# Moving a partial sum two places later in a hand-ordered scan kernel, and fetching one of its inputs a group earlier

## The chip, the cores and the metric

The kernel runs on one NeuronCore of a Trainium2 chip. A NeuronCore has five engines that run their own instruction streams and meet only at semaphores: TensorE (PE, matrix multiplies and transposes into PSUM), VectorE (DVE), ScalarE (ACT), GpSimd (POOL), and SyncE (SP), whose queue issues all the DMA transfers of this kernel. The metric is the device time of one execution in microseconds (us). Three executions of the kernel before gave a median of 11595.92 us (11591.5 to 11607.49). The profile is one further execution, which took 11561.61 us.

## The reference

The input is a batch of eight images of 96 channels, 64 by 64. The first layer is a vision state-space block: layer norm, a projection to 192 inner channels with a depthwise convolution, a selective scan over the 4096 pixels in four directions, a gate, a projection back, and a small convolutional branch. The second layer is linear attention and a quantized feed-forward part. Nearly all the time lies in the scan, which for each of 8 images, 4 directions, 192 channels and 16 states runs 4096 steps:

```python
def step(h, inp):
    u_t, d_t, b_t, c_t = inp
    dA = jnp.exp(d_t[..., None] * A)
    h = dA * h + (d_t * u_t)[..., None] * b_t[:, :, None, :]
    y = jnp.einsum('bkdn,bkn->bkd', h, c_t)
    return (h, y)
...
y = out_y[:, 0] + inv_y[:, 0] + wh_y + invwh_y      # the four directions, added
```

So a scan output is a sum over 16 states, and the final `y` is a sum over four directions (row order, column order, and both reversed). Everything before and after the scan (norms, convolutions, gate, attention, feed-forward) is the "lane" work below.

## The kernel before, in words

**Units, groups, jobs.** Images are taken in four pairs p (NP = 4). A pair has 384 channels, three tiles T of 128 (T = 0, 1: one image each; T = 2: the last 64 channels of both). A job is one pair, one direction k, one chunk of CH = 1024 pixels and one tile T: 192 jobs. A job has four groups j, each of 32 channels; a group g has four units q, each of 128 partitions holding 32 channels by 4 states. That is 768 groups and 3072 units. The first pair takes the directions in the order k = 0, 2, 1, 3, the other pairs 1, 3, 0, 2. Directions 2 and 3 are the reversed ones.

**What a group does.** The names are those of the profile's tiles:

- `spread(g)`: two 128x512 matmuls copy 32 channels of `du` (delta times u) to 128 partitions in the PSUM tile `pu`. There is one `pu`, so the matmuls of group g+1 wait until VectorE has read `pu` for group g.
- `weave(g)`: in three of four groups of T = 0 and in all of T = 1, eight 128x128 transposes of tiles `turned` make the scan input of unit 0 directly in the PSUM tile `pb0`. The `turned` tiles are made by ScalarE: 32 multiplications 128x128 a job, issued in `spin(job)`.
- `decay(u)`: ScalarE's exponential `da`, 128x1024, one a unit; four buffers.
- `scan(u)`, called for pairs of units (q = 0 and q = 2): VectorE multiplies `pu` by `bm` into `pb` (not for a woven unit), then runs two scans of 128x1024 into a tile `hc`; POOL copies the carry and multiplies `hc` by `cm`, in place, 128x2048. There are four `hc` buffers, so two groups' worth.
- `total(g)`: the partial sum. 16 matmuls of 32x256 (in the trace 32, as a float32 matmul runs as two passes) add the four states on the partitions of all four units into `yp`, the left half of the PSUM bank `yps`. In the reversed directions (k = 2, 3) a first matmul with the identity adds the sums of the opposite direction, fetched into `prev`; in k = 2 of the pairs 1 to 3 another adds the turned sums of the column directions, fetched into `yet`. ScalarE copies `yp` to `y`, and one DMA (k < 2) or four (k >= 2) store it.
- `before(g)`: the fetches of `prev` (384 in all) and `yet` (144), one buffer each.

**The order is written out by hand.** `InOrder` (L254 to L280; nearly every instruction is recorded from L266) chains every instruction of PE, DVE, ACT and POOL to the one before it on that engine, so each engine runs them in the order of the program's calls. SP issues DMAs in program order too, and blocks where one has to wait for its buffer or its data.

**Slots.** `Slots.run()` is a tick: it runs what is due at this tick, then lets each generator ("lane") of other work take one step. A group has six ticks: one before the scan of the first pair, two after it, and the same for the second pair; a job has 24, and `at` is the tick modulo 24. The ticks of a group are called slots 1 to 6 here. Lanes get PE and ACT time by a budget (`RATE`, 1.4 and 1.25 us a tick). They write to two PSUM banks only, bank 0 (`pg`) and bank 1 (`yps`, shared with `total`); `take` hands out a free bank and keeps bank 1 away from lanes in the ticks between a partial sum and its copy. `steps(job)` prepares the next job: at tick 5 and 6 of each job it uses both banks for the delta projection, each with a softplus on ACT. `left_at`, `there` and `turned` hold back work whose inputs another lane is still making; if an input is missing at the start of a job, the loop runs 24 ticks of lanes alone, with no scan between.

**The order around the change.** The main loop (L1494 to L1543) does, for a group g:

1. slot 1; `scan` of the first pair; fetches of `bm` and `cm` for later units; `decay` for the second pair; `total(g-1)`;
2. slot 2 (the copy of `yp`, `after(1)`), slot 3;
3. slot 4; `scan` of the second pair; fetches; `decay` for the next group's first pair; `spread(g+1)`, `weave(g+1)`;
4. slot 5, slot 6 (the store of `y`, `after(5)`); then in slot 1 of the next group `before(g)`, so that `prev` for `total(g)` is fetched right before it.

So between `pu` of group g and `pu` of group g+1 PE's queue holds: the transposes of g, the lane matmuls of slots 5, 6 and 1, `total(g-1)`, the lane matmuls of slots 2, 3 and 4.

Of the kernel before, what the change touches and what calls it, by code (L numbers as in the profile page):

```python
# [9 lines left out]
F32 = mybir.dt.float32  # L10
# [272 lines left out]
RING, EXTRA = 7, 1  # L283


class Slots:
# [24 lines left out]
    def take(self, pe, act, long=0, first=False):  # L311
        while True:
            at = self.at % 24
            if long:
                if (
                    self.at % 6 in (5, 0)[: 1 + (long == 2)] and min(self.left) > -2
                    and 0 not in self.held and not at <= 6 < at + long and not self.wanted
                ):
                    self.hold(0)
                    self.pay(pe, act)  # L320
                    i = 0
                    return self.banks[i]
            elif first or min(self.left) > 0:
                free = [
                    i for i in range(2)
                    if i not in self.held and self.at > self.last
                    and not (i == 1 and at % 6 in (1, 2)) and at != (5, 4)[i]
                ]
                if free:
                    i = min(free, key=lambda i: self.used[i])  # L330
                    self.hold(i)
                    self.pay(pe, act)
                    return self.banks[i]
            yield
# [40 lines left out]
def phase_b(  # L375
# [8 lines left out]
    with ExitStack() as ctx:  # L384
# [80 lines left out]
        slots = Slots(bank0, yps)  # L465
# [20 lines left out]
        def woven(job):  # L486

            return jobs[job][3] < 2

        def weaves(u):  # L490

            job, j, q = units[u]
            return q == 0 and woven(job) and not (j == 0 and jobs[job][3] == 0)
# [5 lines left out]
        def steps(job):  # L499

            p, k, ci, c, T, at = where(job)
            if T == 0:

                sts[job // 3] = gp.tile([80, 512], F32, name="st")
                r0, r1 = 64 + R * (k // 2), 32 * (k // 2)
                for i, hs in enumerate(halves):
                    for b in range(2):
                        for to, n, r in ((32 * i + R * b, R, r0), (64 + 8 * i + 4 * b, 4, r1)):
                            nc.sync.dma_start(
                                sts[job // 3][to : to + n, :],  # L510
                                xd_d[k % 2][2 * p + b][r : r + n, at][:, hs],
                            )
            dtw = gp.tile([32 + 2 * R, 128], F32, name="dtw")
            for i in range(2):
                nc.sync.dma_start(dtw[32 * i : 32 * i + 2 * R, :], a["dtw"][:, k, T, :])
            dus[job] = gp.tile([128, CH], F32, name="du", bufs=2)
            nc.sync.dma_start(dus[job], xi_d[k % 2][p][T][:, at])
            yield
            while slots.at % 24 != 5:
                yield  # L520
            dl = gp.tile([128, CH], F32, name="turned", bufs=RING)
            for i, hs in enumerate(halves):
                bank = slots.banks[1 - i]
                assert 1 - i not in slots.held
                slots.hold(1 - i)
                slots.pay(0.9, 2.5)
                rows = slice(32 * i, 32 * i + 2 * R)
                pe.matmul(bank, dtw[rows, :], sts[job // 3][rows, :], start=True, stop=True)
                se.activation(dl[:, hs], bank, AF.Softplus, bias=dtb[:, k, T : T + 1])
                slots.give(bank)  # L530
                if i:
                    exps()
                else:
                    yield
            ge.tensor_mul(dus[job], dus[job], dl)
            yield from wait(2)
            nc.sync.dma_start(dl_d[k][p][T][:, at], dl)
            if woven(job):
                assert slots.spun is None
                slots.spun = spin(job)  # L540
            yield

        def spin(job):


            turns[job], b, slots.wanted = [], jobs[job][3], True
            dt = gp.tile([128, 8, 128], F32, name="turned", bufs=RING)
            for i in range(2):
                bank = yield from slots.take(0.6, 0.6, first=True)
                for x in range(4):  # L550
                    pe.transpose(
                        bank[:, 128 * x : 128 * x + 128],
                        dus[job][:, 512 * i + 128 * x : 512 * i + 128 * x + 128],
                        ident,
                    )
                se.copy(dt[:, 4 * i : 4 * i + 4, :], bank)
                slots.give(bank)
                yield
            if b == 0:
                bts[job // 3] = gp.tile([128, 4, 2, 8], F32, name="bt", bufs=2)  # L560
                bank = yield from slots.take(0.5, 0.3, first=True)
                for x in range(4):
                    pe.transpose(
                        bank[:, 16 * x : 16 * x + 16],
                        sts[job // 3][64:80, 128 * x : 128 * x + 128],
                        ident[64:80, 64:80],
                    )
                se.copy(bts[job // 3], bank[:, 0:64])
                slots.give(bank)
                yield  # L570
            bt, slots.wanted = bts[job // 3], False
            nxt = slots.at
            while len(turns[job]) < 4:
                n, at = len(turns[job]), slots.at % 24
                if slots.at < nxt or (job and woven(job - 1) and n >= EXTRA and 6 < at < 17):
                    yield
                    continue
                nxt = slots.at + 3
                slots.pay(0.0, 2.4)
                t = gp.tile([128, 2, 128, 4], F32, name="turned", bufs=RING)  # L580
                for i in range(2):
                    for m in range(4):
                        x, c = 2 * n + i, 4 * b + m
                        scale = bt[:, x % 4, x // 4, c : c + 1]
                        se.mul(t[:, i, :, m], dt[:, x, :], scale)
                turns[job].append(t)
                yield

        def weave(g):

# [803 lines left out]
        def spread(g):  # L1394
            job, j, _ = units[4 * g]
            for hs in halves:
                pe.matmul(pu[:, hs], sel[:, j, :], dus[job][:, hs], start=True, stop=True)
# [29 lines left out]
        def before(g):  # L1427


            job, j, _ = units[4 * g]  # L1430
            p, k, ci, c, T, at = where(job)
            if k >= 2:
                prevs[g] = wp.tile([128, 256], F32, name="prev", bufs=1)
                nc.sync.dma_start(prevs[g], ya_d[k % 2][p][T][c, j])
            if k == 2 and p > 0:
                assert p in turned
                yet[g] = wp.tile([128, 256], F32, name="yet", bufs=1)
                nc.sync.dma_start(
                    yet[g],
                    ys_d[0][p][T][32 * j : 32 * j + 32, at].rearrange("r (i x) -> i r x", i=4),  # L1440
                )

        def total(g):
# [30 lines left out]
                        y[32 * i : 32 * i + 32, :],  # L1474
                    )

            slots.after(1, lambda: se.copy(y, yp))
            slots.after(5, store)

        slots.first = steps(0)  # L1480
        while not slots.idle():
# [12 lines left out]
        for u in range(0, n, 2):  # L1494
            g, q = divmod(u, 4)
            if q == 0:
                if g % 4 == 0:
# [11 lines left out]
                            slots.lanes.append(columns(p))  # L1509
                    if p == NP - 1 and k == 2:  # L1510
                        if ci == 0 and T == 1:
                            assert not slots.lanes
                            slots.lanes += [last_gate(), last_rest(0), last_rest(1)]
                        if ci > 0 and T == 0:
                            left_at[ci - 1] = slots.at + 15
                    if job < len(jobs):
                        p, k, ci, c, T, at = where(job)
                        while (p, k % 2, c) not in there:
                            for _ in range(24):
                                slots.run()  # L1520
                        slots.first = steps(job)
# [7 lines left out]
                weights(v, 1)  # L1529
            for v in range(u + 2, min(u + 4, n)):  # L1530
                decay(v)
            if q == 2:
                if g + 1 < n // 4:
                    spread(g + 1)
                    if weaves(4 * g + 4):
                        weave(g + 1)
            elif g > 0:
                total(g - 1)
            slots.run()
            slots.run()  # L1540
            if q == 2:
                slots.after(1, lambda g=g: before(g))
        slots.run()  # L1543
        slots.run()
# [501 lines left out]
```

## Time and profile before

| | |
|---|---|
| median of three runs | 11595.92 us |
| profiled execution, device time | 11561.61 us |
| its span, first to last instruction | 11559.5 us |
| DVE busy | 10092.0 us (87%) |
| POOL busy | 8645.6 us (75%) |
| PE busy (weight loads apart) | 8426.8 us (73%) |
| ACT busy | 7949.4 us (69%) |
| DMA queue, share of 16 engines | 49.6% |
| granted TensorE clock, mean | 0.824 |
| first and last scan start | 224.4 and 11224.9 us |

Each row of the page's fifth part is one kind of instruction on one engine: its tiles as out<-in, its count, its busy time in all and the mean of one, then the engine's idle time just before such instructions, with what ended it. The list of waits sums the same idle time by who waited for whom. In the timeline a line is a run of like instructions: start, length, engine, name, and in brackets the idle time before it.

### The profile page before, as it was taken

What the parts mean: (1) busy time and instruction counts of PE and PEld (TensorE: products, weight loads), DVE (VectorE), ACT (ScalarE), POOL (GpSimd) and SP (SyncE); (2) the same over time, 40 slices, a digit from 0 to 9 for tenths busy, and PEclk for the clock granted to TensorE, in tenths of its full rate; (3) what the DMA queues carried; (4) which work ended last, traced back from release to release, by engine and by line L of the source; (5) the groups of instructions that cost most, each with busy time, mean ns of one, the idle gap of its engine ahead of it and who ended that gap; (6) DMA issues with size and microseconds to landing.
All of it is one profiled execution on the core that took longest, in us unless ns stands there. A gap on an engine that the chain in (4) does not pass through costs nothing. (4 is left out here: it accounts for less than half of the span.)

```text
span 11559.5 us, 135952 instructions
## 1 busy us (share of the span) xinstructions
PE 8426.8 (73%) x44332; PEld 3637.9 (31%) x44332; DVE 10092.0 (87%) x6202; ACT 7949.4 (69%) x13591; POOL 8645.6 (75%) x3961
## 2 busy tenths in 40 slices
PE   7867787666687777766677787777767766666778
PEld 3323333222233333333233333333322333222333
DVE  4898999999788899978988889997998989899874
ACT  3657776555777777768777777666876767875664
POOL 2687778777877778877777777878777878877760
PEclk8877887777788888878788888888888888877889
DMA  3454544544645556564444455656444655544551
GB/s 117 141 195 157 160 155 169 174 132 145 202 148 162 161 157 199 180 201 151 147 143 142 149 166 158 204 172 201 154 148 152 163 162 176 183 143 134 165 150 38
DMA packets 902259, 1836.80 MB, mean 159 GB/s; under 512 B 248990, under 2 KB 422239, under 8 KB 894511
## 3 DMA queue, kind: packets, MB, share of 16 engines
q1 hardware_dynamic: 901550, 1828.11, 49.6%
q8 instruction: 352, 5.77, 0.2%
q14 instruction: 357, 2.92, 0.1%
HBM read 1407.23 MB, written 420.42 MB: 158 GB/s over the span
## 5 line engine op out<-in xcount | busy, mean ns | idle before, releaser
L266 POOL TENSOR_TENSOR hc<-hc,cm 128x2048 f32<-128x2048 f32 x1536 | 6970.2, 4538 | 729.4 <-DVE hc L266 410.5
L266 DVE TENSOR_TENSOR_SCAN hc<-da,carry,pb 128x1024 f32<-128x1024 f32 x2304 | 5274.9, 2332 | 259.0 <-ACT da L266 244.6
L266 DVE TENSOR_TENSOR pb<-pu,bm 128x1024 f32<-128x1024 f32 x2624 | 3101.8, 1221 | 796.4 <-PE pu L266 733.6
L266 ACT ACTIVATE da<-dl,c_alog 128x1024 f32<-128x1024 f32 x3072 | 3356.4, 1141 | 120.6 <-DVE hc L266 116.2
L266 PE MATMUL yp<-hc,c_add 128*32 128x256 f32 x24576 | 1989.3, 467 | 1028.5 <-POOL hc L266 801.6
L266 PE MATMUL pu<-du,c_sel 128*128 128x512 f32 x3072 | 1969.5, 775 | 486.3 <-DVE pb L266 485.4
L266 DVE TENSOR_TENSOR_SCAN hc<-da,pb 128x1024 f32<-128x1024 f32 x768 | 1711.6, 2271 | 92.8 <-ACT da L266 84.8
L266 PEld LDWEIGHTS yp<-hc,c_add 128*32 128x32 f32 x24576 | 812.7, 128 | 2227.6 <-POOL hc L266 1068.4
L266 ACT ACTIVATE turned<-turned,bt 128x128 f32<-128x128 f32 x4096 | 1321.1, 509 | 0.0
L266 POOL COPY carry<-hc 128x2 f32<-128x2 f32 x1152 | 215.6, 187 | 1296.4 <-DVE hc L266 1221.9
L266 PEld LDWEIGHTS pu<-du,c_sel 128*128 128x128 f32 x3072 | 688.9, 241 | 1405.3 <-issue 707.5
L266 ACT COPY y<-yp 128x256 f32<-128x256 f32 x768 | 280.9, 366 | 1177.1 <-PE yp L266 1173.4
L266 POOL TENSOR_TENSOR u<-u,u 96x512 f32<-96x512 f32 (+1 forms) x474 | 595.1, 1261 | 212.0 <-ACT u L266 207.1
L266 ACT ACT_TABLE_LOAD x566 | 726.2, 1283 | 34.9 <-DMA cb<-y 13.9
L266 ACT COPY u<-pg 128x512 f32<-128x512 f32 (+5 forms) x492 | 270.7, 550 | 592.4 <-PE pg L266 520.8
L266 PE MATMUL yp<-prev,ident 128*128 128x256 f32 x768 | 312.3, 495 | 481.5 <-DMA prev<-ya 288.9
L266 PEld LDWEIGHTS pb<-ident,turned 128*128 128x128 f32 x3584 | 483.4, 158 | 352.5 <-issue 237.3
L266 POOL TENSOR_TENSOR du<-du,turned 128x1024 f32<-128x1024 f32 x192 | 454.2, 2366 | 164.2 <-ACT turned L266 164.0
L266 PE MATMUL pb<-ident,turned 128*128 128x128 f32 x3584 | 528.4, 296 | 13.3 <-DVE hc L266 13.2
L266 PEld LDWEIGHTS yp<-prev,ident 128*128 128x128 f32 x768 | 156.9, 233 | 785.6 <-issue 291.0
L266 ACT COPY u<-yp 96x512 f32<-96x512 f32 (+6 forms) x252 | 138.8, 551 | 362.0 <-PE yp L266 264.3
L266 PE MATMUL pg<-ain,wmain 96*128 96x512 f32 x792 | 375.2, 613 | 6.3 <-ACT u L266 4.5
(350 smaller groups left out, 8591.2 us busy)
## 6 DMA issues: line engine op xcount, KB each, us to landing
dl<-dl SPq DMA_DIRECT2D x768, 512.0 KB
bm<-xd SPq DMA_DIRECT2D x512, 512.0 KB
cm<-xd SPq DMA_DIRECT2D x512, 512.0 KB
du<-xi SPq DMA_DIRECT2D x192, 512.0 KB
dl<-turned SPq DMA_DIRECT2D x192, 512.0 KB
ya<-y SPq DMA_DIRECT2D x384, 128.0 KB
prev<-ya SPq DMA_DIRECT2D x384, 128.0 KB
xi<-u SPq DMA_DIRECT2D x152, 256.0 KB
```

Source lines behind the costliest of these rows:

```text
L266: op(*args, **kw)
```

## The change

`total(g-1)` is called at the end of the first half of group g, behind slot 3 and not in front of slot 2. The copy of `yp` comes two slots after it and not one (slot 5), the store six and not five (slot 3 of the next group). `before(g)` is called in slot 4 of group g, right behind `total(g-1)`, and not in slot 1 of group g+1. The bank rules follow: bank 1 is kept from lanes in ticks 3, 4 and 5 of six, not in 1 and 2, and the delta projection at tick 5 and 6 takes bank 0 first, not bank 1. The 32 multiplications of a woven job are issued by fours, one four a tick (one every second tick for T = 0), not by eights every third tick. Two loops that run lanes alone are added: before k = 2 of a pair if its `turned` sums are not there, and before the last pair's T = 1 of k = 2 if lanes are left.

```diff
@@ Slots.take
-                    and 0 not in self.held and not at <= 6 < at + long and not self.wanted
+                    and 0 not in self.held and not at <= 5 < at + long and not self.wanted
...
-                    and not (i == 1 and at % 6 in (1, 2)) and at != (5, 4)[i]
+                    and not (i == 1 and at % 6 in (3, 4, 5)) and at != (4, 5)[i]
@@ steps(job)
-                bank = slots.banks[1 - i]
-                assert 1 - i not in slots.held
-                slots.hold(1 - i)
+                bank = slots.banks[i]
+                assert i not in slots.held
+                slots.hold(i)
@@ spin(job)
-            nxt = slots.at
-            while len(turns[job]) < 4:
-                n, at = len(turns[job]), slots.at % 24
-                if slots.at < nxt or (job and woven(job - 1) and n >= EXTRA and 6 < at < 17):
-                    yield
-                    continue
-                nxt = slots.at + 3
-                slots.pay(0.0, 2.4)
-                t = gp.tile([128, 2, 128, 4], F32, name="turned", bufs=RING)
-                for i in range(2):
-                    for m in range(4):
-                        x, c = 2 * n + i, 4 * b + m
-                        scale = bt[:, x % 4, x // 4, c : c + 1]
-                        se.mul(t[:, i, :, m], dt[:, x, :], scale)
-                turns[job].append(t)
-                yield
+            for x in range(8):
+                while job and woven(job - 1) and x >= 2 * EXTRA and 6 < slots.at % 24 < 17:
+                    yield
+                if x % 2 == 0:
+                    t = gp.tile([128, 2, 128, 4], F32, name="turned", bufs=RING)
+                slots.pay(0.0, 1.2)
+                for m in range(4):
+                    c = 4 * b + m
+                    scale = bt[:, x % 4, x // 4, c : c + 1]
+                    se.mul(t[:, x % 2, :, m], dt[:, x, :], scale)
+                if x % 2:
+                    turns[job].append(t)
+                yield
+                if b == 0:
+                    yield
@@ before(g)
-                assert p in turned
@@ total(g)
-            slots.after(1, lambda: se.copy(y, yp))
-            slots.after(5, store)
+            slots.after(2, lambda: se.copy(y, yp))
+            slots.after(6, store)
@@ the main loop
-                            assert not slots.lanes
+                            while slots.lanes:
+                                for _ in range(24):
+                                    slots.run()
...
+                    while k == 2 and p > 0 and p not in turned:
+                        for _ in range(24):
+                            slots.run()
...
-            if q == 2:
-                if g + 1 < n // 4:
-                    spread(g + 1)
-                    if weaves(4 * g + 4):
-                        weave(g + 1)
-            elif g > 0:
-                total(g - 1)
+            if q == 2 and g + 1 < n // 4:
+                spread(g + 1)
+                if weaves(4 * g + 4):
+                    weave(g + 1)
             slots.run()
             slots.run()
-            if q == 2:
+            if q == 0:
+                if g > 0:
+                    total(g - 1)
                 slots.after(1, lambda g=g: before(g))
```

## The prediction

> **What bounds the kernel now.** First the page's busy times, then its costliest groups, then the list of waits, then one stretch of the timeline. From the page:
>
> ```profile
> L266 DVE TENSOR_TENSOR_SCAN hc<-da,carry,pb 128x1024 f32<-128x1024 f32 x2304 | 5274.9, 2332 | 259.0 <-ACT da L266 244.6
> L266 DVE TENSOR_TENSOR pb<-pu,bm 128x1024 f32<-128x1024 f32 x2624 | 3101.8, 1221 | 796.4 <-PE pu L266 733.6
> L266 DVE TENSOR_TENSOR_SCAN hc<-da,pb 128x1024 f32<-128x1024 f32 x768 | 1711.6, 2271 | 92.8 <-ACT da L266 84.8
> ```
>
> VectorE does the scans and sets the pace: these rows are 10088 of its 10092 us. The last column is what can be won at all: 796.4 + 259.0 + 92.8 = 1148 us of idle time, 734 of it for `pu`, 329 for `da`. Two stretches of the page by windows show both ends, DVE busy 199 us of 200 where lanes are few, 144 where the fetches of `yet` are added:
>
> ```profile
> core 0: us, PE busy (x) PEld busy (x) DVE busy (x) ACT busy (x) POOL busy (x), PEclk, DMA share, GB/s
> 2400.00:2600.00 200.00, 120.57 (x684) 52.40 (x684) 199.06 (x116) 106.24 (x161) 153.82 (x66) 0.75 0.39 129
> 5000.00:5200.00 200.00, 147.19 (x725) 61.68 (x726) 143.84 (x85) 116.77 (x205) 146.24 (x90) 0.81 0.59 192
> ```
>
> The list of waits says who is late. PE, in order, stands before the partial sum `yp` for POOL's `hc` and for `prev` and `yet`; ACT stands before the copy `y`:
>
> ```profile
> ACT y L266 <- PE yp L266: 1173.4, 412, 12.1
> PEld yp L266 <- POOL hc L266: 1068.4, 427, 12.2
> PE yp L266 <- POOL hc L266: 801.6, 320, 11.7
> DVE pb L266 <- PE pu L266: 733.6, 282, 11.3
> DVE hc L266 <- ACT da L266: 329.4, 190, 26.8
> PE yp L266 <- DMA prev<-ya: 288.9, 51, 16.7
> PE yp L266 <- DMA yet<-ys: 48.2, 27, 7.3
> ```
>
> The timeline of one late group ties these together:
>
> ```profile
> 5000.28 4.45 DVE L266 TENSOR_TENSOR_SCAN hc<-da,pb 128x1024 f32<-128x1024 f32 x2
> 5001.33 1.22 PE L266 MATMUL yp<-prev,ident 128*128 128x256 f32 x2 [3.15 <-DMA prev<-ya]
> 5003.55 1.22 PE L266 MATMUL yp<-yet,ident 128*128 128x256 f32 x2 [1.00 <-DMA yet<-ys]
> 5004.70 3.01 PE L266 MATMUL yp<-hc,c_add 128*32 128x256 f32 x32
> 5007.65 1.10 PE L266 MATMUL pg<-u,c_centre 96*96 96x512 f32 x2
> ...
> 5009.91 1.10 PE L266 MATMUL yp<-u,mean 96*96 96x512 f32 x2 [1.17 <-ACT u L266]
> ...
> 5010.85 1.88 PE L266 MATMUL pu<-du,c_sel 128*128 128x512 f32 x4
> ...
> 5012.77 1.23 DVE L266 TENSOR_TENSOR pb<-pu,bm 128x1024 f32<-128x1024 f32 x1 [8.03 <-PE pu L266]
> ```
>
> PE stood 4.15 us for the two fetches, ran the sum, then 3.2 us of lane work (slots 2 to 4), and only then `pu`; DVE had been done since 5004.73. PE's stop lies in front of lane work that needed none of what it waited for.
>
> **The change part by part.** *PE.* From the two programs' orders, each lane matmul priced by the timeline's 0.43 us between passes of 512 columns, a group has 4.19 us of lane matmuls on PE in both. Before, 2.49 stand ahead of the sum and 1.70 between sum and `pu`; after, 3.87 and 0.32. So 1.38 us a group, 81% of what lies between, goes in front of the sum, into the stop. I read for every group from the trace's records: when PE was free ahead of the sum, when the sum ended, when `pu` began, when POOL's `hc` ended. 294 groups have a late `pu` (734 us). In these, from the start of the first pair's scans, PE was free at 2.3 us, `hc` ended at 2.8, the sum at 7.65 though its matmuls need some 2.0 (32 passes took 1.93 at 9389.81), `pu` began at 11.9, and DVE was done at 11.8. The new start of `pu` is then the later of (free + 81% of the lane stretch + 2.0, and 0.4 to 0.7 for the identity matmuls) and (`hc` end + 1.1 for the second half), plus 19% of the lane stretch. Per group, and never more than its wait, this gives 390 us of the 734; in 124 groups the wait goes wholly. Bounds: 0, if the lane matmuls moved ahead find their own inputs late, and 734.
>
> The discount: the lane stretch of a late group is 4.24 us long with 3.27 busy, so 0.97 waits, mostly for ACT; run earlier, they may wait longer. A quarter of the gain, 100 us; ends 0 and 294 x 0.97 x 0.81 = 231.
>
> What is late next is PE itself: in 127 groups lanes, sum, `pu` and transposes add to more than the 12.88 us that a group takes where DVE is never idle (48 groups in 618 us, 2226 to 2845), by 160 us together. That stays in any order.
>
> *The fetches (SP).* `prev` and `yet` are asked for a group's length ahead and not in the same slots; their 289 + 48 us on PE are part of the 390. 384 and 144 transfers move three slots up SP's queue; each waits there until `total(g-1)` has read its buffer. SP's wait for that is 456.1 us in 213 cases before, 2.1 each. Queued behind it are `bm`, `cm`, `dl`, lane loads and stores; POOL waits for `cm` (103.2 us, 41 times) and ACT for lane loads. They are needed a pair or more later (6.7 us in a quiet group), so I take 0, ends -50 and +100.
>
> *ACT.* The copy of `yp` goes behind the two `da` of the next first pair, where it stood ahead of them. In 35 of the 200 scans that waited for `da` ACT had just stood for `yp`, worth 34 us; more is due to lane copies that stood for PE. I take -50, ends 0 and -150. Who waits for the copy: lane matmuls in bank 1, now first in slot 6, with `pu` and slot 5 between. The store moves with it, 1 or 4 DMAs a group three slots down SP's queue; nobody reads them for several groups: 0. If that cover were gone it would show as `prev` waits again.
>
> *Multiplications by fours.* 4096 before and after. For T = 0 the last four come in slot 3 of the next job and not in slot 23, one slot ahead of the transposes that read them. These stand behind `pu` and have a `pb` product and two scans (5.9 us) for cover, so 0; without it 64 jobs x 1.3 us = 83.
>
> *Banks.* Lanes get bank 1 in three ticks of six, not four; their finish slips. Counted in the program: the kernel before runs 24 ticks without a scan once, before job 6 (DVE idle 26.8 us for `da`, then 6.1); the new one does not, but does so before job 132, where `turned` sums are missing. There PE has 23.3 us of work. So -33 and +25: -8.
>
> *The clock.* The four passes of `pu` took 1.88 us at 5010.85 and 3.51 at 9382.97, behind a stop of 16.65 us. By groups: with a stop at the sum under 1 us they take 2.19 us on average, with 3.4 to 6 us 3.08, with more 2.44. I take -25, ends 0 and -95 (0.89 us in 106 late groups with a stop over 3.4). [...]
>
> The sum: -390 + 100 - 50 - 8 - 25 = -373. The profiled execution took 11561.6 us, so 11189. The median of the runs stands 34 above it: **11,223 us**, 3.2% less. Everything else (counts of DVE, POOL and DMA instructions, the tail behind 11227 us) is the same.
>
> **The rivals.** *A: moved lanes wait where they now stand.* PE then reaches the sum later than POOL. For: 1641 lane matmuls ahead of the sum wait for ACT in the new order, 999 in the old. Against: the 642 stood ahead of `pu` before too. With the discount at 231 and no ACT gain: -390 + 231 - 8 = -167, about 11,430.
>
> *B: slower.* The sum is now glued to `pu`, behind all lane work: groups with over 7 us of lane matmuls ahead of the sum go from 11 to 144 (nine-tap convolutions above all). If each of these 144 ends its sum later by more than 390/144 = 2.7 us than my row-by-row shift says, the gain is gone; at 4 us it costs 576 - 373 = +203, 11,800. For: a wait of PE for ACT in such lanes is 1.8 us (PEld pg for ACT u, 401.6 us in 222). Against: 7.7 us of lanes, one such wait, sum and `pu` still end within some 1.5 us of DVE's scans.
>
> *C: more goes.* A group on time makes POOL's and ACT's next steps earlier too, so that only PE's own 160 us of the `pu` waits stay: -574 + 100 - 50 - 8 - 25 = -557, 11,039. For: where lanes are few DVE does stand still no more than 1 us of 200. Against: groups heavy with lanes follow one another.
>
> *D: no change.* `pu` comes earlier and DVE waits for `da` or `cm` in its place: 11,596. ACT is busy 69% and POOL 75%, against it.
>
> **How the numbers follow.** Forecast (11,100 to 11,330) 0.48, C (below 11,100) 0.16, A (11,330 to 11,572) 0.22, D 0.04, B 0.10. A measurement here cannot tell under 0.2%, 23 us, from no change. Faster: 0.48 + 0.16 + 0.22 = 0.86; same 0.04; slower 0.10. The range takes C to 11,000 (0.06 lies below), A to 11,560 (some 0.14 above).
>
> **What would show it.** DVE's wait for `pu` falls from 734 us to 300 to 450, and stays at 650 or more if A or B holds. PE's waits before `yp` for `prev` and `yet` go to nearly nothing. PE's waits for POOL `hc` fall by half or more. ACT's wait for `yp` falls far below 1173. DVE's 26.8 us stop at 521 is gone, and one of 15 to 35 us appears near job 132. The forecast is wrong if PE's waits for ACT ahead of the sum grow by as much as those for POOL shrink, or if SP, held at `prev`, brings `cm` or lane loads late.

## The result

The changed kernel takes 11785.2 us (11777.43 to 11793.01), the kernel before 11601.7 us beside it: a ratio of 1.0159 (95% interval 1.0141 to 1.0176). It is 1.6% slower, 184 us, where 373 us less were forecast. The profiled execution took 11793.0 us.

### The profile page after: what moved, and what is told of

Its sections match the earlier page's. It is cut to its first block, busy times and chain, and to the rows that moved or that the text cites. A ratio compares the mean times of both kernels' runs of the same rounds, so it can differ in the third digit from the quotient of the medians.

```text
span 11791.2 us, 135866 instructions
## 1 busy us (share of the span) xinstructions
PE 8565.9 (73%) x44332; PEld 3696.0 (31%) x44332; DVE 10087.3 (86%) x6202; ACT 7950.5 (67%) x13591; POOL 8645.2 (73%) x3961
## 5 line engine op out<-in xcount | busy, mean ns | idle before, releaser
L266 PE MATMUL yp<-hc,c_add 128*32 128x256 f32 x24576 | 2047.6, 484 | 588.0 <-POOL hc L266 400.0
L266 PE MATMUL pu<-du,c_sel 128*128 128x512 f32 x3072 | 1875.0, 741 | 638.1 <-DVE pb L266 637.8
L266 PEld LDWEIGHTS yp<-hc,c_add 128*32 128x32 f32 x24576 | 859.2, 134 | 1780.0 <-issue 857.1
L266 ACT ACTIVATE turned<-turned,bt 128x128 f32<-128x128 f32 x4096 | 1373.8, 514 | 0.2
L266 PEld LDWEIGHTS pu<-du,c_sel 128*128 128x128 f32 x3072 | 638.4, 228 | 1510.2 <-DVE pb L266 824.1
L266 ACT COPY u<-pg 128x512 f32<-128x512 f32 (+6 forms) x528 | 293.2, 555 | 817.5 <-PE pg L266 723.4
L266 PE MATMUL yp<-prev,ident 128*128 128x256 f32 x768 | 344.5, 541 | 232.3 <-ACT u L266 117.7
L266 PE MATMUL pg<-ident,du 128*128 128x128 f32 x740 | 197.0, 420 | 375.0 <-POOL du L266 332.1
L266 ACT ACTIVATE turned<-pg,c_dtb 128x512 f32<-128x512 f32 x192 | 132.0, 688 | 406.3 <-PE yp L266 399.7
L266 PE MATMUL pg<-ain,wmix 96*128 96x512 f32 x792 | 353.2, 594 | 0.0
```

Source lines behind the costliest of these rows:

```text
L266: op(*args, **kw)
```

## The profile after

VectorE's three rows of the page, which were shown of before:

```profile
L266 DVE TENSOR_TENSOR_SCAN hc<-da,carry,pb 128x1024 f32<-128x1024 f32 x2304 | 5274.1, 2332 | 190.2 <-ACT da L266 174.0
L266 DVE TENSOR_TENSOR pb<-pu,bm 128x1024 f32<-128x1024 f32 x2624 | 3102.3, 1221 | 1083.5 <-PE pu L266 1052.2
L266 DVE TENSOR_TENSOR_SCAN hc<-da,pb 128x1024 f32<-128x1024 f32 x768 | 1711.2, 2270 | 103.7 <-ACT da L266 95.2
```

The work is the same; the idle time is not. For `da` it fell by 60 us, for `pu` it rose from 734 to 1052, and the sum over these rows, 1148 before, is 1377: 229 us more, of the 232 that the span gained (11559.5 to 11791.2). So the loss is late `pu`, and the question is what PE did. The list of waits after:

```profile
DVE pb L266 <- PE pu L266: 1052.2, 367, 25.9
PEld yp L266 <- POOL hc L266: 596.3, 249, 12.6
PE yp L266 <- POOL hc L266: 400.0, 162, 6.8
PEld pg L266 <- POOL du L266: 387.2, 56, 10.8
PE pg L266 <- POOL du L266: 332.1, 56, 9.3
PEld yp L266 <- POOL du L266: 297.6, 74, 8.7
PE yp L266 <- POOL du L266: 231.0, 68, 8.4
ACT y L266 <- PE yp L266: 61.2, 55, 5.6
PE yp L266 <- DMA prev<-ya: 38.8, 13, 5.5
```

The stops that the change aimed at are gone or halved: PE for POOL's `hc` from 802 to 400 us, for `prev` from 289 to 39, ACT for `yp` from 1173 to 61. New is PE's wait for POOL's `du`: 332 + 231 us, where the list of before has only

```profile
PE pg L266 <- POOL du L266: 59.6, 66, 3.6
```

(A PEld row and a PE row are the weight load and the matmul of the same stop.) Sorted by the group in which PE stood, all of the 503 us added lie in the groups j = 1 of the jobs T = 1 and T = 2, where `spin` puts the transposes of the next job's `du` into slots 2 and 3. One such group in the timeline of the changed kernel:

```profile
2286.86 0.69 PE L266 MATMUL pg<-st,dtw 12*128 12x512 f32 x1
...
2288.04 4.53 POOL L266 TENSOR_TENSOR hc<-hc,cm 128x2048 f32<-128x2048 f32 x1
2288.60 0.68 ACT L266 ACTIVATE turned<-yp,c_dtb 128x512 f32<-128x512 f32 x1
...
2289.88 4.45 DVE L266 TENSOR_TENSOR_SCAN hc<-da,pb 128x1024 f32<-128x1024 f32 x2
...
2292.52 2.36 POOL L266 TENSOR_TENSOR du<-du,turned 128x1024 f32<-128x1024 f32 x1
...
2294.94 1.11 PE L266 MATMUL yp<-ident,du 128*128 128x128 f32 x4 [4.09 <-POOL du L266]
...
2295.84 1.06 PE L266 MATMUL pg<-ident,du 128*128 128x128 f32 x4
...
2296.49 4.45 DVE L266 TENSOR_TENSOR_SCAN hc<-da,pb 128x1024 f32<-128x1024 f32 x2
2296.73 1.22 PE L266 MATMUL yp<-prev,ident 128*128 128x256 f32 x2
...
2297.88 3.05 PE L266 MATMUL yp<-hc,c_add 128*32 128x256 f32 x32
...
2302.88 1.98 PE L266 MATMUL pu<-du,c_sel 128*128 128x512 f32 x4
...
2304.90 1.23 DVE L266 TENSOR_TENSOR pb<-pu,bm 128x1024 f32<-128x1024 f32 x1 [3.96 <-PE pu L266]
```

POOL's queue has `hc` (ready at 2292.57), and behind it `du` (2294.88). The sum needs only `hc`. In the new order it stands behind the transposes, which need `du`; PE idles 4.09 us, and only then runs transposes, sum and `pu`, one after the other. The same group in the kernel before:

```profile
2292.96 3.64 PE L266 MATMUL yp<-hc,c_add 128*32 128x256 f32 x32
2294.37 2.37 POOL L266 TENSOR_TENSOR du<-du,turned 128x1024 f32<-128x1024 f32 x1
...
2296.80 0.66 PE L266 MATMUL pg<-ident,du 128*128 128x128 f32 x4 [0.19 <-POOL du L266]
...
2297.29 0.60 PE L266 MATMUL yp<-ident,du 128*128 128x128 f32 x4
...
2298.48 1.98 PE L266 MATMUL pu<-du,c_sel 128*128 128x512 f32 x4 [0.59 <-DVE pb L266]
```

There the sum runs while POOL makes `du`, the transposes wait 0.19 us, and `pu` waits for VectorE, not VectorE for `pu`. The mean over the 127 groups of this kind says the same (worked out from the trace's records, us from the start of the first pair's scans):

| | before | changed |
|---|---|---|
| POOL `hc` of the last pair ends | 2.49 | 2.57 |
| POOL `du` ends | 5.58 | 5.46 |
| transposes of `du`, first start to last end | 6.56 to 8.20 | 5.54 to 7.86 |
| sum | 2.65 to 6.15 | 8.73 to 11.82 |
| `pu` of the next group | 8.63 to 10.99 | 12.37 to 14.37 |
| DVE's scans end; its next work starts | 11.52; 11.93 | 11.39; 14.42 |

Before, PE ran the sum while POOL made `du`. POOL's `du` came as late, but the sum filled that time. DVE's wait behind these groups rose from 52 to 385 us.

## Experiments

The theory is this: the sum's old place covered the wait for `du`, and the early fetch and the fours are no loss. The rival is the prediction's own B: the sum behind long chains of lane matmuls, in any group. Four kernels were run first. All edits are against the kernel named.

**Put the sum back in j = 1 alone** (changed kernel):

```diff
+            if q == 0 and g % 4 == 1:
+                total(g - 1)
             slots.run()
             slots.run()
             if q == 0:
-                if g > 0:
+                if g > 0 and g % 4 != 1:
                     total(g - 1)
@@ total
-            slots.after(2, lambda: se.copy(y, yp))
+            slots.after(1 if g % 4 == 0 else 2, lambda: se.copy(y, yp))
@@ Slots.take
-                    and not (i == 1 and at % 6 in (3, 4, 5)) and at != (4, 5)[i]
+                    and not (i == 1 and (at in (7, 8) if 6 < at < 13 else at % 6 in (3, 4, 5)))
+                    and at != (4, 5)[i]
```

> The changed kernel with the sum back in its old place, ahead of slots 2 and 3, only in the second group of each job (j = 1), where the transposes of `du` stand in slots 2 and 3. Theory 1 (the sum now stands behind transposes that wait for POOL's `du`): DVE's waits for `pu` fall by the 334 us that they rose after the j = 1 groups, from 1052 to some 720, PE's waits for POOL `du` from 559 to under 150, time about 11,440. Rival (the sum behind long chains of lane matmuls anywhere, the prediction's B): a quarter of the groups is put back, so a quarter of the rise at most, 11,700 or more.

11,473 us (ratio to before 0.9892, 0.9877 to 0.9906): 312 us off the changed kernel, and 1.1% faster than the kernel before. The edit puts back 192 groups, as it takes in the 64 groups j = 1 of T = 0, which have no such transposes; behind those DVE's wait for `pu` is 49 us and not 81, behind the 127 it is 68 and not 385. DVE's waits for `pu` are 728 us in all. The list of waits has 60 us of PE for `du`, as before:

```profile
DVE pb L266 <- PE pu L266: 728.2, 279, 23.2
PE pg L266 <- POOL du L266: 60.0, 70, 4.2
```

Theory 1 holds, and rival B (11,700 or more) falls.

**Transposes of a constant** (changed kernel): `dus[job][:, 512 * i + 128 * x : ...]` in `spin` becomes `sel[:, x, :]`.

> The changed kernel with the same transposes in the same places, but of a constant and not of `du`, so that they wait for nothing on POOL (the scan inputs of the woven units are wrong by that). Theory 1: it is the wait that costs, not the place of the work, so PE's waits for POOL `du` go to 0, DVE's for `pu` to 700 to 760, time about 11,430. If the work itself in front of the sum costs (1.6 us in 128 groups, at most 205 us in all) and the wait does not, PE's stops move to the sum, and the time stays at 11,700 or more.

11,662 us (1.0052, 1.0037 to 1.0067), 123 us off the changed kernel and not 350. PE waits for `du` no more, but it waits for ACT in its place:

```profile
DVE pb L266 <- PE pu L266: 902.7, 341, 11.5
PE pg L266 <- ACT turned L266: 346.6, 214, 8.9
```

The same row has 127 us in the changed kernel. DVE's wait behind the 127 groups fell from 385 to 266 us, and no further. Of the 347 us, 214 are transposes that wait for a copy out of their own bank: in 56 of these groups both fours of transposes go to one bank in the changed order, and the second has to wait until ACT has copied the first away. 37 are transposes that wait for the softplus. So `du` is one link of a chain (projection, softplus, `du`, transposes, copies), and taking one link away leaves the rest in front of the sum. To take the wait for `du` alone away is worth 123 us, to put the sum back ahead of the chain 312.

**The early fetch alone** (kernel before): `if q == 2:` becomes `if q == 0:` in front of `slots.after(1, lambda g=g: before(g))`.

> The kernel before with the fetches of `prev` and `yet` alone moved, to slot 4 of their group. PE's waits for them fall from 337 us to under 50. In groups with a late `pu` these were 289 us, with nothing else moved ahead of the sum. If a stop of PE in a late group is worth its length: DVE's waits for `pu` from 734 to some 500, time 11,330 to 11,420. If other waits take its place, as in the changed kernel, where 250 us of these stops went and `pu` was no earlier: 11,540 to 11,600.

11,464 us (0.9883, 0.9868 to 0.9898), 140 us less. PE's wait for `prev` is 37 us. In 637 groups of the other kinds DVE's wait for `pu` went from 682 to 576 us. A stop taken away with nothing moved in front of the sum does pay, though less than the bracket given (the time is 44 us over it): of 289 us of such stops in late groups, 106 were DVE's.

**The fours alone** (kernel before, with the new loop of `spin`).

> The kernel before with the multiplications by fours alone. No time in the multiplications themselves (4096 before and after); as lanes finish sooner in this order, the 24 ticks without a scan before job 6 are not run at all, so DVE's stop of 26.8 and 6.1 us is gone: about 11,570. If the last four, one slot ahead of the transposes that read them, are late: PE waits of transposes for `turned` grow by some 80 us, 11,650.

11,500 us (0.9917, 0.9901 to 0.9934), 104 us less. The stretch without a scan before job 6 (33 us) is gone as expected; DVE's waits for `da` are 285 us and not 329, 27 of the fall being the stop of that stretch, and those for `pu` are 729, about the same. By the profiled executions (11561.6 and 11502.2) the gain is 59 us, and most of it is these waits; the rest of the 104 lies between profiled runs and medians and is not explained. Nothing was lost.

So both small parts gain alone, and the sum's move must cost more than the whole loss. The next four kernels took it apart.

**The sum's move alone** (changed kernel, with the old loop of `spin` and `before(g)` back in slot 1).

> The changed kernel without the early fetch (back in slot 1 of the next group) and without the multiplications by fours: the sum moved, with its copy, store and bank rules, and nothing else. Measured alone, the early fetch was worth -140 us and the fours -104. Theory 1 with parts that add: 11,785 + 140 + 104 = some 12,030. If the sum's move takes the fetch's gain too (it leaves the fetch two slots more time by itself): some 11,890. If the move were not what costs: under 11,785.

11,828 us (1.0214, 1.0198 to 1.0229), under both numbers but 43 us over the changed kernel. With the sum two slots later a late fetch has more time: PE's waits for `prev` and `yet` are 128 us, without the early fetch, where they were 337. So the move takes away most of the stops that the early fetch would have, and the fetch and the fours, 244 us alone, are worth 43 together in this order. DVE's stop before job 6 is there too, 43 us long and not 27.

**Early fetch and fours, the sum in its old place** (kernel before).

> The kernel before with the early fetch and the fours, the sum in its old place: the changed kernel without its one move. Theory 1: the two gains stand beside each other, 11,605 - 140 - 104 = some 11,360, over 400 us under the changed kernel and 110 under the one with the sum put back in j = 1 alone. If the move helps outside j = 1, as its shorter waits for POOL suggest: this one is no faster than that one, 11,470 or more.

11,392 us (0.9840, 0.9824 to 0.9856): 1.6% faster than before, 3.3% faster than the changed kernel, the best of all. Its page:

```profile
L266 DVE TENSOR_TENSOR_SCAN hc<-da,carry,pb 128x1024 f32<-128x1024 f32 x2304 | 5272.7, 2330 | 189.5 <-ACT da L266 175.6
L266 DVE TENSOR_TENSOR pb<-pu,bm 128x1024 f32<-128x1024 f32 x2624 | 3099.5, 1219 | 689.9 <-PE pu L266 621.1
```

and two rows of its waits, the first larger than in any kernel so far:

```profile
PE yp L266 <- POOL hc L266: 869.5, 348, 9.3
DVE pb L266 <- PE pu L266: 621.1, 275, 11.6
```

PE stands longer for POOL than before (870 us against 802) and less than half as long in the changed kernel (400), which is slower.

**The sum late in j = 1 of T = 1 and 2 alone** (kernel before; bank 1 closed in ticks 3 and 4 there):

```diff
+        def late(g):
+            return g % 4 == 1 and jobs[g // 4][3]
...
-            elif g > 0:
+            elif g > 0 and not late(g):
                 total(g - 1)
             slots.run()
             slots.run()
+            if q == 0 and g > 0 and late(g):
+                total(g - 1)
```

> The kernel before with the sum behind slot 3 only in the groups j = 1 of the jobs T = 1 and 2, where the transposes of `du` stand in slots 2 and 3: the suspected cause alone, in 128 of 768 groups. Theory 1: DVE's waits for `pu` behind these groups from 52 to some 385 us, the rest as before, and no stretch of 24 ticks without a scan (33 us): some 11,900. Rival (the cause is lane work in all groups): under 11,700.

11,802 us (1.0193, 1.0176 to 1.0210). The edit in 128 of 768 groups alone makes the kernel as slow as the whole change does. Its waits:

```profile
DVE pb L266 <- PE pu L266: 1033.1, 385, 24.1
PE yp L266 <- POOL du L266: 482.5, 75, 10.4
```

Behind these groups `pu` is 339 us late, 46 under the number given; that is about half of the 98 us by which the time is under its own.

**The sum late where it had seemed to help** (early fetch and fours, sum behind slot 3 in j = 0 of T = 0 and j = 2 of T = 2).

> Early fetch and fours, and the sum behind slot 3 only in j = 0 of T = 0 and j = 2 of T = 2, where the waits for `pu` fell most in the changed kernel (136 to 18 and 59 to 14 us). If that was the sum's place: some 40 us under the kernel with early fetch and fours alone. If it was the early fetch (with it alone they are 58 and 25): the same within 25 us.

11,399 us (0.9845, 0.9830 to 0.9859), the same as without (11,392). Behind the two kinds of groups `pu` is 74 and 10 us late, without the edit 48 and 5. What fell there in the changed kernel was mostly the early fetch's doing.

**The late sum with an early `du`.** In the kernel with the sum late in j = 1 alone, the delta projection goes to ticks 3 and 4, so that `du` stands ahead of the second pair's `hc` on POOL; the same is done in the best kernel. These two differ in more than the sum's place, as the first has neither the early fetch nor the fours.

```diff
-            while slots.at % 24 != 5:
+            while slots.at % 24 != 3:
...
             nc.sync.dma_start(dl_d[k][p][T][:, at], dl)
             if woven(job):
+                yield from wait(2)
@@ Slots.take
-                    and 0 not in self.held and not at <= 6 < at + long and not self.wanted
+                    and 0 not in self.held and not at <= 4 < at + long and not self.wanted
-                    and at != (5, 4)[i]
+                    and at != (3, 2)[i]
```

> The kernel with the sum late in j = 1 alone, and in it the delta projection two ticks earlier (ticks 3 and 4), so that POOL's `du` stands ahead of the second pair's `hc` in its queue and not behind it; the transposes stay in front of the sum in 108 of the 127 groups (in 19 half of them). Theory 1 (the wait for `du`): it ends some 5 us sooner, PE's waits for POOL `du` fall from some 620 us to under 150, DVE's for `pu` behind these groups from 339 to under 120, time from 11,801 to some 11,570. If ScalarE's part of the chain (softplus, the copies of the transposes, one bank) takes over, as with the constant transposes: those `pu` waits stay over 230, 11,700 or more.

> The kernel with early fetch and fours, the sum in its old place, and the same earlier delta projection. Theory 1: with the sum in front, `du` was hidden behind it (PE waited 72 us for POOL in lanes of these groups), so nothing much is won: 11,390 within 40. If a `du` of 2.4 us ahead of `hc` delays the sum and with it `pu`: 11,450 or more.

11,730 us (1.0130, 1.0115 to 1.0145) and 11,639 us (1.0044, 1.0027 to 1.0061). The waits went the way of the theory: with an early `du` PE's waits for POOL's `du`, 618 us with a late one, are 60, most of them in the second of these rows:

```profile
PEld yp L266 <- POOL du L266: 73.5, 32, 5.1
PE yp L266 <- POOL du L266: 40.9, 27, 4.8
```

`pu` behind the j = 1 groups is 142 us late and not 339, where under 120 was expected. The times did not: in the best kernel the early projection costs 247 us by itself (11,392 to 11,639). There POOL's queue stands for the softplus in front of `hc`:

```profile
POOL du L266 <- ACT turned L266: 329.5, 115, 10.2
PE yp L266 <- POOL hc L266: 1202.9, 410, 8.6
```

(73 and 870 us without it.) What the late sum costs can't be read from these two times, as the early fetch and the fours differ too; it can be read from DVE's waits for `pu` behind the 127 groups, where those two count for little (52 us before, 72 with both). With a late `du` the late sum takes them from 52 to 339 us, with an early one they are 94 with the sum in its old place and 142 with the late one: 287 us against 48. In the other groups the early projection adds some 125 us of such waits with either sum (549 to 674, 670 to 792), and so the kernel with the late sum won only 72 us by it (11,802 to 11,730). It looks like the same mistake on another engine: an instruction with a late input, put ahead of one whose input was there.

**The 24 ticks without a scan, alone** (early fetch and fours, `slots.run()` 24 times before job 132).

> The kernel with early fetch and fours (11,392), and 24 ticks of lanes without a scan before job 132, where the changed kernel and the one with the sum put back in j = 1 have them: the price of such a stretch, and the fair partner of the latter (11,473), which differs from it then only in the sum's place in the other 640 groups. From DVE's stops there in those two (54 and 60 us): 11,440 to 11,455, which leaves 20 to 30 us to the sum's place in 640 groups. At the prediction's 25 us: 11,417. If the sum's place elsewhere costs by itself, this stretch is short, and the time 11,400 or less.

11,410 us (0.9843, 0.9826 to 0.9860): 18 us more, which is not clear of the 19 us by which the kernel before differs from one set of runs to another. DVE does stop,

```profile
7698.36 4.46 DVE L266 TENSOR_TENSOR_SCAN hc<-da,pb 128x1024 f32<-128x1024 f32 x2 [37.56 <-ACT da L266]
```

but the lane work done there need not be done later: by the traces this kernel is 10 us ahead of the best one before the stretch, 37 behind it two groups on, 21 after twelve and 3 after 72, so that 13 of 47 us are left. My expected numbers took the stop for the price.

With this partner the parts are: early fetch and fours -194 (11,586 to 11,392), the 24 ticks +18, the sum late in 576 groups, all but j = 1, with its bank rules +63 (11,410 to 11,473), in the 192 groups j = 1 +312 (11,473 to 11,785). Together +199; the measured difference was 184. Each kernel set against the kernel before of its own set of runs, the steps are -194, +13, +50 and +315. In the 63, or 50, lies a longer stop in the stretch before job 132: 31.8 and 27.7 us where the partner has 37.6.

**Why the other groups gained nothing.** PE's stops sorted by whether the next `pu` was late (637 groups outside the 127, from the trace's records, us in all):

| | before, late (258) | before, on time (379) | changed, late (248) | changed, on time (389) |
|---|---|---|---|---|
| at the sum, for POOL | 171 | 556 | 9 | 389 |
| at the sum, for a DMA | 289 | 38 | 10 | 33 |
| in lanes, for ACT | 426 | 195 | 598 | 172 |

Of 727 us that PE stood for POOL in these groups, 556 were in groups where nobody waited for it. Of the 171 that mattered, 162 went, and 172 came back as waits of lane matmuls for ACT. Before, the sum stood between two steps of lane work, and ACT emptied the bank meanwhile; behind all of them, it fills no such wait. The same in the sum's move alone: 727 to 389 for POOL, 622 to 953 in lanes for ACT. 102 late groups came in time (-240 us), 92 others became late (+231). That this exchange is what costs the 50 to 63 us is argued from these sums; no run isolates it.

## Why the prediction was wrong

- **"PE's stop lies in front of lane work that needed none of what it waited for."** The step that failed. It was read from one group, whose lanes were norms, and even there one of the lane matmuls shown waited 1.17 us for ACT. Slots 2 and 3 also hold the transposes of the next job, whose input is made by POOL behind the very `hc` that the sum waits for. In the order of the queues this can be read without a run: the sum depends on an instruction ahead of the one that the moved work depends on. It cost 312 us (11,785 with it, 11,473 with the sum put back in j = 1), and the discount for "lane matmuls that find their own inputs late", 100 us with 231 as its end, was the term that should have held it.
- **The 390 us, group by group.** The working moved each group's lane stretch as a block with its old length into PE's stop. It took the inputs of that block for ready. In the 637 other groups the waits for `pu` fell by 40 us (682 to 642), and the early fetch alone had given 106. Outside j = 1 the sum's own move lost 50 to 63 us of time.
- **Rival B** had the sign and nearly the time (11,800), with the wrong place: it looked for nine-tap convolutions, in 144 groups with more than 2.7 us each. It was 127 groups, behind which DVE waits 3.0 us each (11.39 to 14.42) and waited 0.4 before, and what stood ahead of the sum was short but late.
- **The fetches** were right in mechanism: 289 to 39 us, POOL's waits for `cm` 103 and 98, so there is no sign that anything behind them on SP was hurt. Alone they are worth 140 us.
- **ACT** was right in its waits (1173 to 61 for `yp`, `da` 329 to 269) and `da` moved by about the term of -50. That this was the copy's doing is not shown: the early fetch and the fours alone, with the copy in its old place, bring `da` to 274, the 269 has the stop of 47 us before job 132 in it, and no run moves the copy by itself.
- **The fours** at 0 were worth -104 alone, 59 by the profiled executions: `da` fell by 45 us, 27 of it the stop of the lost stretch. Without a stretch before job 6 already by them alone, they also hold the -33 that stood under the banks.
- **The 24 ticks**, priced at 25 against 33: DVE's stop was 47 us, while the net price of such a stretch, measured elsewhere, was 13 to 18 us, no more than the noise.
- **The clock** was taken for a gain; the granted clock fell from 0.824 to 0.811. Around the stop of 4.09 us shown above it was 1.00 from 2286.6 to 2293.3, 0.50 from 2293.4 to 2300.1 and 1.00 again from 2300.2. At 0.50 four transposes took 1.06 to 1.11 us, where eight take 1.04 at 1.00 in the kernel before (at 9386.32), and the sum, most of it at 0.50, 3.05 instead of 1.93. The changed kernel's trace has this clock in steps of 3.41 us, each at 1.00 or 0.50. In the step before the fall shown PE had been busy for 0.90 us. Before the 548 falls between 300 and 11,100 us it had been busy for 1.07 us in the median, and only 70 of them came behind a step without a matmul; in the steps at 1.00 that another at 1.00 followed, the median is 2.64. So by these traces a new stop of PE cost more than its length, though no run isolates the clock: a four of these transposes that ran through took 1.06 us on average, in the kernel before 0.79. The forecast took -25, with 0.89 us a group as its end. That figure is a difference over all groups; among the groups with a late `pu` the passes of `pu` took 2.3 us with a stop under 1 us and 2.5 with one of 3.4 to 6, so there was little to win.

## What to carry to other kernels

Before an instruction is moved behind others on an in-order engine, each of those others must be asked what it waits for and where that stands in its own engine's queue; if it is later than the moved one's input, the move takes a filling out of one wait and adds the two up, which cost 312 us here. Idle time on an engine that is not the bottleneck is worth winning only in the groups where somebody was late, here 171 of the 727 us that PE stood for POOL outside those 127: sort the waits by that first. When a change has several parts, the parts that shorten a wait without moving work in front of other work are worth running alone; here they gave 1.6%, and the rest of the change took 3.5% away (11,392 to 11,785).

## What the runs showed of the hardware that was not expected

The prices that were isolated are matters of queue order. Two sizes were not expected: 247 us for setting one softplus and one POOL product two ticks earlier, with the bank rules that go with it, and 13 to 18 us, no more than the noise, for a stretch in which VectorE stands for 38. And at the stop of 4.09 us the granted clock went from 1.00 to 0.50 when PE's last matmul had ended 2.5 us before, behind a step of 3.41 us in which PE had been busy for 0.90.
